# The last node batch of a graph convolution begins two steps earlier, in finer pieces

## The chip, the cores and the metric

The kernel runs on one core of a Trainium2 chip. The metric is the time of one execution in device microseconds, given as the median of several runs. The engines are TensorE (PE, with its weight loads PEld), VectorE (DVE), ScalarE (ACT), GpSimd (POOL) and SyncE (SP), which issues most DMAs. Each engine works its own instructions in order; semaphores join them.

## The reference

A graph network layer: two convolutions over 200,000 edges and 6,250 nodes with 128 features, then attention over the same edges. The edges are sorted by target node.

```python
def mesh_conv(x, src, dst, ea, w1, b1, g, bt, w2, b2):
    m = jnp.concatenate([x[dst], x[src], ea], axis=-1) @ w1 + b1
    m = jax.nn.silu(group_norm(m, g, bt))
    m = m @ w2 + b2
    out = jax.ops.segment_sum(m, dst, num_segments=n)
    cnt = jax.ops.segment_sum(jnp.ones((dst.shape[0],), m.dtype), dst, num_segments=n)
    return out / jnp.clip(cnt, 1.0)[:, None]

h = mesh_conv(x, src, dst, edge_attr, c1_w1, ...)                 # convolution 1
h = jax.nn.silu(group_norm(h, n1_g, n1_b))
h = h + (jax.nn.silu(t_emb) @ tm_w + tm_b)
h = mesh_conv(h, src, dst, edge_attr, c2_w1, ...)                 # convolution 2
h = jax.nn.silu(group_norm(h, n2_g, n2_b)) + x
...                                                               # attention over the edges
```

The targets are drawn as the whole part of 6250 u^2, u uniform from 0 to 1, and sorted.

## The kernel before

**Chunks and steps.** The edges are cut into 196 chunks of 1024 (the last holds 384). A convolution goes over them in the 197 steps of `pipeline`. In each step several chunks are under way. `fetch` of chunk n+2 loads its part of the table of targets (`pk`) and of the relative targets (`ohT`, one DMA for two chunks) on SP, and gathers the table of sources with eight indirect DMAs on POOL into one of four buffers `g`. `products` of chunk n+1 multiplies on TensorE (L1166, into `m`). `first` of chunk n adds the gathered rows on VectorE (L1173), squares on ScalarE (L1175) and reduces the squares on VectorE (L1177). `compared` of chunk n+2 makes the one-hot rows on ScalarE (L685, L686). `second` of an earlier chunk normalises it with three VectorE multiplies and adds (L1188, L1191, L1192), applies SiLU on ScalarE (L1193) and sums the edges by node on TensorE (L1198, into `u`); two masked copies on ScalarE (L1203) and an add on VectorE (L1208) bring the sums into the table `U` in a later step. The root of the variances (ScalarE L1184, reciprocal on VectorE L1274) is taken for two chunks together, which makes odd and even steps differ, and for one chunk at a time in the last steps.

**Node batches.** When all edges of a window of nodes are summed, the nodes themselves can be worked. A batch is four windows of 128 nodes, and `conv_nodes` is its work, as a generator: each `yield` ends its part of one step, and `go_on` resumes it once in each step. `plan_batches` lists the steps in which batches begin, every eighth step, and beside each the chunk whose window number bounds what is finished then. In convolution 1 there are 14 batches, in steps 81, 89, ..., 169, 177, 185. In order, a batch scales the sums (five VectorE instructions, L948 to L955), transposes and copies them (L898, L908), multiplies by the convolution's second weight (L914), adds the bias and squares (L963, L919), reduces the variance (L967), waits for the shared root, scales by it (L925), then idles. After that it transposes again and applies the SiLU (`turned`, L898 and L906), and for each of two weights multiplies (L914), copies (L1007) and stores to the tables `b_d` and `a_d` of the next convolution (L1002, L1012). All batches but the last have six empty steps between L925 and the transposes; the last has none.

Every product and transpose of a batch goes through one PSUM bank, `nd`, which has a single buffer.

**Order.** The order of the instructions on VectorE, ScalarE, TensorE and SP is the order in which the program writes them: `in_order` pins it. In the last 24 steps of a convolution (`early`, n over 172) a batch's part stands ahead of `compared` and `second` in its step, except the parts for variance and scaling, which stand at its end. `products` of the next chunk comes before the batch's part, `second` after it.

**The end of a convolution.** After step 196, `mend` redoes batches that the plan couldn't cover (a loop of zero passes where there are none), and `last_nodes` does the nine last windows of nodes. The next convolution's gathers read the whole table `b_d` and so wait for these nodes.

Of the kernel before, what the change touches and what calls it, by code (L numbers as in the profile page):

```python
# [11 lines left out]
AF = mybir.ActivationFunctionType  # L12
# [19 lines left out]
BN = 4  # L32
# [18 lines left out]
def kernel(ctx: ExitStack, tc: tile.TileContext, x, src, dst, eat, w, out):  # L51
# [9 lines left out]
    nc = tc.nc  # L61
# [106 lines left out]
    NWD = max(0, (NW - 8) // BN * BN)  # L168
    fix_i = {i: const.tile([1, 2], I32, name=f"fix_i{i}") for i in (1, 3)}

    def by_node(table_d, wi, m):
        return table_d[wi * P:(wi + m) * P, :].rearrange("(w p) c -> p w c", p=P)
# [24 lines left out]
    with tc.tile_pool(name="node0", bufs=1) as np_, tc.tile_pool(name="prep", bufs=1) as pp, \  # L197
# [3 lines left out]
        A = h0  # L201
# [43 lines left out]
        for a in range(0, NW, 4):  # L245
            m = min(4, NW - a)
# [12 lines left out]
            tp = pst.tile([P, 4, P], FP, name="tp")  # L259
            for i in range(m):  # L260
                nc.tensor.transpose(tp[:, i, :], A[:, a + i, :], ident)
            tT = np_.tile([P, 4, P], FP, name=f"tT{a}")
# [4 lines left out]
            b = rt.tile([P, 4, D], FP, name="b0")  # L267
# [21 lines left out]
        for a, (m, tT) in keep.items():  # L289
# [3 lines left out]
            b = rt.tile([P, 4, D], FP, name="a0")  # L293
            nc.scalar.copy(b[:, :m, :], o[:, :m, :])
            last = nc.sync.dma_start(out=by_node(a_d[1], a, m), in_=b[:, :m, :])
# [47 lines left out]
    cols = {n: hpc.tile([P, 1], FP, name=f"k_{n}") for n in ("n1_g", "n1_b", "n2_g", "n2_b", "tm_b")}  # L343
# [12 lines left out]
    def steps_of(i):  # L356


        ends, due, n = {}, {}, 0
        for m in spread(i):  # L360
            ends[n + m] = list(range(n, n + m))
            due.setdefault(n + m + (i == 3 or n < NCH - SOON), []).extend(ends[n + m])
            n += m
        waiting, todo, left = [], [], NCH
        while left:
            n = len(todo)
            waiting += due.get(n, ())
            steps = min([m for m in due if m > n], default=n + 1) - n
            k = -(-len(waiting) // steps)
            todo.append(waiting[:k])  # L370
            waiting = waiting[k:]
            left -= k
        return ends, todo

    def plan_batches(i):

        ends, todo = steps_of(i)
        out, done = [], 0
        for n, now in enumerate(todo):
            done += len(now)  # L380
            if n % 8 == (4 if i == 3 else 1) and n > (40 if i == 3 else 80) and n + 6 < NCH \
                    and (i == 3 or n + 5 in ends):
                out.append((n, max(done - 3, 0)))
        return out if NWD else []

    plans = {1: plan_batches(1), 3: plan_batches(3)}
    plans[2] = plans[1]
    at_i = {i: const.tile([1, max(len(plans[i]), 1)], I32, name=f"at_i{i}") for i in (1, 3)}

    for i in (1, 3):  # L390
        plans[i] = plan_batches(i)
# [494 lines left out]
    class Nodes:  # L886
# [11 lines left out]
                nc.tensor.transpose(tp[:, j, :], t[:, j, :], ident)  # L898
            return tp[:, :m, :]

        def turned(self, t, m, tag="x", silu=None):

            tp = self.in_bank(t, m)
            out = self.tile(m, tag)
            if silu:
                nc.scalar.activation(out, tp, AF.Silu, bias=cols[f"{silu}_b"], scale=cols[f"{silu}_g"])  # L906
            else:
                nc.scalar.copy(out, tp)  # L908
            return out

        def times(self, tT, m, rhs):
# [23 lines left out]
    def rows_of(table_d, w, m):  # L935
        at = bass.ds(w * P, m * P) if not isinstance(w, int) else slice(w * P, (w + m) * P)
        return table_d[at, :].rearrange("(w p) c -> p w c", p=P)

    def span(w, m):
        return bass.ds(w, m) if not isinstance(w, int) else slice(w, w + m)  # L940

    def conv_nodes(b, i, w, m, idle=0, last=False):


        at = span(w, m)
        c = b.pool.tile([P, 2, BN], FP, name="n_c")
        if i == 1:
            nc.vector.tensor_scalar(c[:, 0, :m], U[:, at, D], 1.0, None, ALU.max)  # L948
            nc.vector.tensor_scalar(c[:, 1, :m], U[:, at, D], 1.0, None, ALU.min)
            nc.vector.reciprocal(c[:, 0, :m], c[:, 0, :m])  # L950
            nc.vector.tensor_copy(cnt[:, :, at], c[:, :, :m])
        else:
            nc.vector.tensor_copy(c[:, :, :m], cnt[:, :, at])
        st = b.tile(m, "x")
        nc.vector.tensor_tensor(st, U[:, at, :D], c[:, 0, :m, None].to_broadcast([P, m, D]), ALU.mult)  # L955
        yield
        tT = b.turned(st, m)
        yield
        o = b.times(tT, m, squares[f"c{i}_w2"])
        yield  # L960
        A = b.tile(m, "A")
        for j in range(m):
            nc.vector.scalar_tensor_tensor(  # L963
                A[:, j, :], rows[f"c{i}_b2"], c[:, 1, j:j + 1], o[:, j, :], ALU.mult, ALU.add)
        sq = b.squares_of(A, m)
        yield "var"
        nc.vector.tensor_reduce(b.var(), sq, AX.X, ALU.add)  # L967
        yield "root"
        if i == 1 or last:
            b.inverse(A, m)  # L970
            h0T = b.in_bank(h0[:, at, :], m) if i == 2 else None
            yield
            for _ in range(idle + 2 * (idle > 0)):
                yield
            tT = b.turned(A, m, "t", silu=f"n{i}")
            if i == 2:
                nc.vector.tensor_tensor(tT, tT, h0T, ALU.add)
        else:
            b.scaled(A, m, f"n{i}_g", f"n{i}_b")
            yield  # L980
            nc.scalar.activation(A, A, AF.Silu)
            yield
            nc.vector.tensor_tensor(A, A, h0[:, at, :], ALU.add)
            yield

            for _ in range(idle):
                yield
            nc.sync.dma_start(out=rows_of(h2_d, w, m), in_=A)
            tT = b.turned(A, m, "t")
        yield  # L990
        if i == 1:
            ends = ((wab[2][:, D:], None, b_d[2]), (wab[2][:, :D], None, a_d[2]))
        else:
            ends = ((qkv_t[:, 1, :], "kb", kv_d[:, :D]), (qkv_t[:, 2, :], "vb", kv_d[:, D:]),
                    (qkv_t[:, 0, :], "qb", a_d[3]))
        done = None
        for rhs, bias, d_ in ends:
            o = b.times(tT, m, rhs)
            if bias:
                yield  # L1000
            if done:
                nc.sync.dma_start(out=rows_of(done[0], w, m), in_=done[1])  # L1002
            t = b.tile(m, "o")
            if bias:
                nc.vector.tensor_tensor(t, o, rows[bias][:, None, :].to_broadcast([P, m, D]), ALU.add)
            else:
                nc.scalar.copy(t, o)  # L1007
                yield
            done = d_, t
        if bias:  # L1010
            yield
        nc.sync.dma_start(out=rows_of(done[0], w, m), in_=done[1])  # L1012
        if i == 2 and last:
            nc.sync.dma_start(out=rows_of(h2_d, w, m), in_=b.turned(tT, m))
# [58 lines left out]
    def nodes_of(b, i, w, m, hx=None):  # L1073
        return attention_nodes(b, w, m, hx) if i == 3 else conv_nodes(b, i, w, m, last=hx is not None)
# [53 lines left out]
    def conv(i):  # L1128
# [6 lines left out]
        with ExitStack() as es:  # L1135
# [17 lines left out]
            nodes = Nodes(np_of(np_, "A", "o"), lambda: nd.tile([P, BN, D], FP, name="nd", tag="nd"))  # L1153
# [56 lines left out]
            class Stage:  # L1210
                ahead, soon = 2, True
                sums, late, roots, next = [], [], False, 0
                var, j, sd = None, 0, None
# [68 lines left out]
                def batch(self, j):  # L1282
                    w = nc.values_load(at_i[1][0:1, j:j + 1], engines=[DVE, SP], min_val=0,
                                       max_val=max(NWD - BN, 0), skip_runtime_bounds_check_because=WHY)
                    for r in conv_nodes(nodes, i, w, BN, idle=4 if j + 1 < len(plans[i]) else 0):
                        self.roots |= r == "root"
                        yield r

# [53 lines left out]
    with ExitStack() as es:  # L1342
# [22 lines left out]
        nodes = Nodes(np_of(pool("np", 1)), bank)  # L1365
# [135 lines left out]
        class Stage:  # L1501
            ahead, soon = 2, False
            sums, late, nb = [], [], None
            lg, j = None, 0
# [98 lines left out]
        n = NW - NWD  # L1603
# [87 lines left out]
```

## Time and profile before

| | |
|---|---|
| time, median of 3 runs | 6164.96 us (6163.35 to 6166.92) |
| the profiled execution's own time | 6177.55 us |
| its span, first to last instruction | 6175.8 us |
| granted TensorE clock, mean | 0.75 |
| busy: VectorE, POOL, PE, ScalarE | 4994.3, 4487.6, 3615.7, 3353.9 us |
| instructions | 68330 |

In the profile, L-numbers are lines of the kernel. A row of a timeline gives start, duration, engine, line, operation, output and inputs, the count, and in brackets how long the engine had been idle before and what ended that. The last edge sums of convolution 1 (L1198) start at 2055.18 us, and the first gather of convolution 2 at 2079.42.

### The profile page before, as it was taken

Reading aid. Unit: us, or ns where it says so; the run is one execution under the profiler, and the core shown is the slowest. Engines: PE = TensorE matmul, PEld = TensorE weight load, DVE = VectorE, ACT = ScalarE, POOL = GpSimd, SP = SyncE. Lnnn points to the kernel's source line nnn. Section 1 sums busy time; section 2 is a strip of 40 time slices with the busy share of each in tenths; the row PEclk is TensorE's granted clock in tenths of the full one; section 3 lists DMA queues with packets and bytes.
Section 4 is the critical chain, followed back from the end, with each engine's and each line's share of the span. In section 5 each row is a group of like instructions: output and inputs, shape, how many; then the busy total and the mean of one; then the engine's idle time right before and its main releaser. Section 6 shows DMA issues by size and latency. Waiting matters only on the chain. (4 is left out here: it accounts for less than half of the span.)

```text
span 6175.8 us, 68330 instructions
## 1 busy us (share of the span) xinstructions
PE 3615.7 (59%) x20941; PEld 3418.9 (55%) x20942; DVE 4994.3 (81%) x7118; ACT 3353.9 (54%) x5295; POOL 4487.6 (73%) x4706
## 2 busy tenths in 40 slices
PE   5555556556556455565565656555655666666555
PEld 4555555555555455555555555544555555555555
DVE  7888888888888578777888888856778888888877
ACT  5666666666666566666666666632333333333354
POOL 5777777777777577777777777757777777777772
PEclk8777667777777677777777787766778777777776
DMA  6444344444433333343344444445566666666652
GB/s 160 116 127 121 96 115 105 102 108 107 107 101 101 80 100 96 100 101 100 102 114 114 109 112 108 112 121 146 152 157 162 165 166 163 163 166 162 165 150 62
DMA packets 391221, 758.87 MB, mean 123 GB/s; under 512 B 89647, under 2 KB 256946, under 8 KB 361441
## 3 DMA queue, kind: packets, MB, share of 16 engines
q0 software_dynamic: 175056, 410.03, 25.9%
q1 hardware_dynamic: 210144, 340.73, 21.0%
q10 hardware_dynamic: 5632, 3.50, 0.2%
q8 instruction: 173, 2.83, 0.2%
q14 instruction: 216, 1.77, 0.1%
HBM read 707.34 MB, written 46.58 MB: 122 GB/s over the span
## 5 line engine op out<-in xcount | busy, mean ns | idle before, releaser
L718 POOL DMA_INDIRECT g<-b_d,src_i x3126 | 2970.9, 950 | 963.4 <-issue 915.5
L1198 PE MATMUL u<-h,oh 128*128 128x129 f32 (+1 forms) x6252 | 1266.3, 384 | 1435.0 <-ACT h L1193 1434.9
L1198 PEld LDWEIGHTS u<-h,oh 128*128 128x128 f32 x6252 | 1169.3, 288 | 1517.1 <-ACT h L1193 1512.6
L718 POOL DMA_INDIRECT g<-kv_d,src_i x1563 | 1490.7, 954 | 494.6 <-issue 446.4
L1166 PE MATMUL m<-pk,ohT 101*128 101x128 f32 x6252 | 943.2, 315 | 206.4 <-DVE h L1173 161.9
L1166 PEld LDWEIGHTS m<-pk,ohT 101*128 101x128 f32 x6252 | 909.7, 231 | 227.3 <-DVE h L1173 180.7
L1173 DVE TENSOR_TENSOR h<-m,g 128x1024 f32<-128x1024 f32 x392 | 476.4, 1215 | 519.4 <-DMA g<-b_d,src_i 496.0
L1452 PE MATMUL us<-v,oh 128*128 128x145 f32 x3126 | 593.1, 359 | 385.4 <-DVE flat L1477 340.6
L1376 PE MATMUL qe<-pk,ohT 101*128 101x136 f32 x3126 | 567.1, 352 | 373.7 <-ACT ebs L1393 364.1
L1452 PEld LDWEIGHTS us<-v,oh 128*128 128x128 f32 x3126 | 549.8, 250 | 425.6 <-DVE flat L1477 239.6
L1376 PEld LDWEIGHTS qe<-pk,ohT 101*128 101x128 f32 x3126 | 525.0, 252 | 406.5 <-ACT ebs L1393 399.8
L1193 ACT ACTIVATE h<-h 128x1024 f32<-128x1024 f32 x392 | 413.0, 1054 | 594.4 <-DVE h L1192 578.9
L1175 ACT ACTIVATE sq<-h 128x1024 f32<-128x1024 f32 x392 | 411.7, 1050 | 527.9 <-DVE h L1173 526.0
L685 ACT ACTIVATE ohT<-ohT,minus_p 96x1024 f32<-96x1024 f32 x588 | 669.2, 1138 | 17.0 <-DMA ohT<-rel_d 16.5
L686 ACT ACTIVATE ohT<-ohT 96x1024 f32<-96x1024 f32 x588 | 619.8, 1054 | 18.7
L1177 DVE TENSOR_REDUCE var<-sq 128x64 f32<-128x1024 f32 x392 | 475.0, 1212 | 104.5 <-ACT sq L1175 104.4
L1191 DVE TENSOR_TENSOR h<-h,cps 128x1024 f32<-128x1024 f32 x392 | 477.1, 1217 | 13.5
L1192 DVE TENSOR_TENSOR h<-h,cps 128x1024 f32<-128x1024 f32 x392 | 477.0, 1217 | 13.4
L733 DVE TENSOR_TENSOR oh<-cps,dm 128x1024 f32<-128x1024 f32 x392 | 474.2, 1210 | 2.1 <-PE u L1198 2.1
L1188 DVE TENSOR_TENSOR h<-h,cps 128x1024 f32<-128x1024 f32 x392 | 473.7, 1208 | 0.0
L1391 DVE TENSOR_TENSOR g<-qe,g 128x768 f32<-128x768 f32 (+1 forms) x391 | 251.1, 683 | 235.0 <-DMA g<-kv_d,src_i 234.6
L1465 ACT ACTIVATE us<-d 128x16 f32<-128x16 f32 x196 | 36.7, 187 | 660.0 <-DVE d L1461 605.6
(286 smaller groups left out, 4270.6 us busy)
## 6 DMA issues: line engine op xcount, KB each, us to landing
ohT<-rel_d SPq DMA_DIRECT2D x291, 768.0 KB
g<-b_d,src_i POOLq DMA_INDIRECT x3126, 2.5
pk<-a_d SPq DMA_DIRECT2D x588, 46.0 KB
g<-kv_d,src_i POOLq DMA_INDIRECT x1563, 3.0
ohT<-in_eat_dram SPq DMA_DIRECT2D x291, 40.0 KB
a_d<-n_o SPq DMA_DIRECT2D x28, 256.0 KB
kv_d<-n_o SPq DMA_DIRECT2D x28, 256.0 KB
n_h<-h_d SPq DMA_DIRECT2D x19, 256.0 KB
```

The lines of the kernel that those rows point to most:

```text
L685: nc.scalar.activation(k.ohT[:WN, :], k.ohT[:WN, :], AF.Square, bias=minus_p[:WN])
L686: nc.scalar.activation(k.ohT[:WN, :], k.ohT[:WN, :], AF.Relu, bias=1.0, scale=-4.0)
L718: h = nc.gpsimd.indirect_dma_start(out=g[:, t, :table_d.shape[1]], out_offset=None, in_=table_d, in_offset=bass.IndirectOffsetOnAxis(ap=k. ...
L733: return nc.vector.tensor_tensor(k.oh[:, :k.nt, :], iota[:, None, :].to_broadcast([P, k.nt, P]), k.dm[:, :, None].to_broadcast([P, k.nt, P ...
L1166: nc.tensor.matmul(k.m[:, t, :], lhsT=lhs[:, t * P:(t + 1) * P], rhs=rhs, start=(j == 0), stop=(j == len(terms) - 1))
L1173: nc.vector.tensor_tensor(k.mt, k.m[:, :n], k.g[:, :n], ALU.add)
L1177: return lambda: nc.vector.tensor_reduce(var[:, at:at + n * H], sq[:, :n].rearrange("p t (g c) -> p (t g) c", c=HD), AX.X, ALU.add)
L1191: nc.vector.tensor_tensor(k.mt, k.mt, over_edges(gam, k.nt), ALU.mult)
L1192: nc.vector.tensor_tensor(k.mt, k.mt, over_edges(bet, k.nt), ALU.add)
L1198: nc.tensor.matmul(k.u[:, 0, :wide], lhsT=k.oh[:, t, :], rhs=k.h[:, t, :wide], start=(t == 0), stop=(t == k.nt - 1))
L1376: nc.tensor.matmul(k.qe[:, t // TB, at:at + DB], lhsT=lhs[:, t * P:(t + 1) * P], rhs=rhs, start=(j == 0), stop=(j == len(terms) - 1))
L1452: nc.tensor.matmul(k.u[:, :wide], lhsT=k.oh[:, t, :], rhs=k.v[:, t, :wide], start=(t == 0), stop=(t == k.nt - 1))
```

## The change

The last batch of convolution 1 begins two steps sooner (183 instead of 185), and the chunk that bounds its window goes back with it (179 instead of 181). Convolution 2 gets its own plan, which is as it was. `idle` becomes 0 for convolution 1's last batch but one, so that its SiLU follows L925 in the next step; in convolution 2 that batch keeps its 4. A new flag `fine`, set for the last batch of convolution 1 alone, adds a yield between the transposes and the SiLU and one between each product and its copy. To make that possible, `turned` loses its SiLU, which becomes `silu_of`.

```diff
@@ plan_batches
+        if i != 1 or len(out) < 2:
+            return out if NWD else []
+        n = out[-1][0] - 2
+        out[-1] = n, max(sum(len(now) for now in todo[:n + 1]) - 3, 0)
         return out if NWD else []
 
     plans = {1: plan_batches(1), 3: plan_batches(3)}
-    plans[2] = plans[1]
+    plans[2] = plan_batches(2)
@@ class Nodes
-        def turned(self, t, m, tag="x", silu=None):
+        def turned(self, t, m, tag="x"):
 
             tp = self.in_bank(t, m)
             out = self.tile(m, tag)
-            if silu:
-                nc.scalar.activation(out, tp, AF.Silu, bias=cols[f"{silu}_b"], scale=cols[f"{silu}_g"])
-            else:
-                nc.scalar.copy(out, tp)
+            nc.scalar.copy(out, tp)
+            return out
+
+        def silu_of(self, tp, m, n):
+            out = self.tile(m, "t")
+            nc.scalar.activation(out, tp, AF.Silu, bias=cols[f"{n}_b"], scale=cols[f"{n}_g"])
             return out
@@ conv_nodes
-    def conv_nodes(b, i, w, m, idle=0, last=False):
+    def conv_nodes(b, i, w, m, idle=0, last=False, fine=False):
...
             for _ in range(idle + 2 * (idle > 0)):
                 yield
-            tT = b.turned(A, m, "t", silu=f"n{i}")
+            tp = b.in_bank(A, m)
+            if fine:
+                yield
+            tT = b.silu_of(tp, m, f"n{i}")
...
             o = b.times(tT, m, rhs)
-            if bias:
+            if bias or fine:
                 yield
@@ Stage.batch of the convolutions
-                    for r in conv_nodes(nodes, i, w, BN, idle=4 if j + 1 < len(plans[i]) else 0):
+                    for r in conv_nodes(nodes, i, w, BN, idle=(0, 4 * i - 4, 4)[min(len(plans[i]) - 1 - j, 2)],
+                                        fine=i == 1 and j + 1 == len(plans[i])):
```

## The prediction

> **What bounds the kernel now.** I read the page first, then the waits of the end of convolution 1 (from 1880 to 2060 us), then the timelines of the engines there, and last the busy times cut at the steps. From the page:
>
> ```profile
> span 6175.8 us, 68330 instructions
> ...
> L718 POOL DMA_INDIRECT g<-b_d,src_i x3126 | 2970.9, 950 | 963.4 <-issue 915.5
> ```
>
> The gathers of both convolutions take (2970.9 + 915.5) / 3126 = 1.24 us apiece on POOL, eight to a chunk, so 9.95 us a chunk. Over the 196 chunks of a convolution that rate sets the pace. The change touches only the end of convolution 1, so I ask what the pace is there. The waits of 1880 to 2060 us (total, times, longest):
>
> ```profile
> POOL g L718 <- issue: 32.9, 108, 0.3
> ACT n_o L1007 <- PE nd L914: 27.7, 6, 6.5
> ...
> ACT n_t L906 <- PE nd L898: 12.0, 2, 6.1
> ```
>
> POOL runs without a break, and VectorE's sum of products and gathered rows (L1173) is not in the list as waiting for a gather. What is there are eight waits of ScalarE for TensorE in the node batches, together 39.7 us. The step rows show what they cost. I cut the time at each start of L1188, the first normalising multiply of a chunk, counting back from the last full chunk (194, begun at 2045.27, step 196). So the 14 rows are steps 181 to 194; the row of step 190 holds two chunks.
>
> ```profile
> 1887.61:1900.75 13.14, 8.58 (x44) 8.34 (x44) 9.10 (x11) 7.06 (x9) 9.79 (x12) 0.63 0.19 54
> 1900.75:1911.78 11.03, 5.26 (x34) 5.07 (x34) 7.97 (x9) 6.54 (x8) 8.59 (x9) 0.81 0.61 157
> 1911.78:1924.97 13.19, 8.82 (x51) 8.62 (x51) 8.34 (x10) 8.05 (x11) 9.84 (x12) 0.76 0.27 74
> 1924.97:1932.40 7.43, 4.21 (x26) 4.02 (x25) 7.36 (x8) 6.32 (x8) 5.60 (x7) 0.73 0.68 154
> 1932.40:1942.33 9.93, 8.19 (x58) 7.76 (x57) 9.36 (x15) 5.87 (x9) 7.49 (x9) 0.85 0.34 81
> 1942.33:1949.76 7.43, 2.44 (x11) 2.44 (x12) 7.36 (x8) 7.30 (x9) 5.60 (x7) 0.72 0.70 159
> 1949.76:1959.10 9.34, 8.58 (x63) 8.20 (x61) 9.27 (x14) 6.13 (x9) 7.21 (x8) 0.86 0.22 63
> 1959.10:1966.54 7.44, 2.58 (x12) 2.58 (x13) 7.37 (x8) 5.67 (x7) 5.61 (x7) 0.74 0.70 170
> 1966.54:1979.48 12.94, 8.38 (x45) 8.14 (x44) 9.10 (x12) 7.06 (x9) 9.82 (x11) 0.63 0.20 55
> 1979.48:1997.11 17.63, 10.08 (x56) 9.59 (x56) 13.86 (x16) 9.82 (x13) 13.33 (x14) 0.70 0.37 103
> 1997.11:2009.71 12.60, 6.80 (x44) 6.37 (x44) 7.93 (x9) 8.85 (x11) 9.46 (x10) 0.76 0.28 77
> 2009.71:2022.20 12.49, 6.72 (x42) 6.53 (x41) 7.93 (x9) 8.17 (x10) 7.56 (x8) 0.77 0.25 68
> 2022.20:2034.17 11.97, 7.26 (x42) 7.07 (x42) 7.92 (x9) 7.10 (x10) 0.00 (x0) 0.79 0.09 25
> 2034.17:2045.27 11.10, 4.79 (x24) 4.30 (x22) 9.55 (x12) 7.18 (x11) 0.00 (x0) 0.65 0.01 2
> ```
>
> Columns: length, then PE, PEld, DVE, ACT, POOL busy. A step without batch work on TensorE and ScalarE takes 7.44 us when even and 9.34 when odd, and there VectorE is full (7.37 of 7.44). Steps 181 to 183 hold the three last pieces of the batch begun at step 169 (transpose and SiLU, first product and copy, second product and copy) and take 13.14, 11.03, 13.19: 3.8, 3.6 and 3.85 us too much. The batch begun at 177 idles and has the same pieces in 189, 190, 191; the one begun at 185 has them in 191, 192, 193. Step 192 on ScalarE shows the mechanism:
>
> ```profile
> 2013.08 0.59 ACT L1007 COPY n_o<-nd 128x512 f32<-128x512 f32 x1 [4.20 <-PE nd L914]
> 2013.56 1.15 ACT L685 ACTIVATE ohT<-ohT,minus_p 96x1024 f32<-96x1024 f32 x1
> 2014.74 1.06 ACT L686 ACTIVATE ohT<-ohT 96x1024 f32<-96x1024 f32 x1
> 2015.71 0.69 ACT L1203 ACTIVATE u<-u,mask 128x129 f32<-128x129 f32 x2
> 2016.41 1.28 ACT L1193 ACT_TABLE_LOAD   x1
> 2017.71 1.06 ACT L1193 ACTIVATE h<-h 128x1024 f32<-128x1024 f32 x1
> 2018.67 1.04 ACT L1175 ACTIVATE sq<-h 128x1024 f32<-128x1024 f32 x1
> 2019.73 1.28 ACT L1184 ACT_TABLE_LOAD   x1
> 2021.03 0.35 ACT L1184 ACTIVATE sd<-var,eps_t 128x64 f32<-128x64 f32 x1
> ```
>
> The copy waits 4.20 us for a product that stands on TensorE behind the chunk's two big matmul groups, and 4.15 us of in-order work (2013.56 to 2017.71) queues behind the copy, ahead of the chunk's SiLU. In step 194, with no such piece, the SiLU waits only for VectorE:
>
> ```profile
> 2037.92 1.06 ACT L1193 ACTIVATE h<-h 128x1024 f32<-128x1024 f32 x1 [1.40 <-DVE h L1192]
> ```
>
> This gives the undisturbed time of a single-chunk step: 2037.92 - 2034.17 = 3.75 from multiply to SiLU, 2022.20 - 2017.71 = 4.49 from SiLU to the next multiply, 8.24 together.
>
> **The change part by part.** By the yields of the code, the batch of 177 (no idle steps now) does its SiLU in 183, its first product and copy in 184, its second in 185. The last batch begins in 183 instead of 185, transposes and copies in 184, multiplies by the convolution's second weight in 185, and adds the bias in 186. The variance follows in 187, the scaling in 188. Its fine pieces are: transposes 189, SiLU 190, product 191, copy 192, product 193, copy 194, last store 195. No ScalarE instruction of it then sits behind a product of its own step.
>
> Taken away. Step 189 falls from 12.94 to 9.34: 3.6. Step 190 loses a piece whose neighbours cost 3.6 (189) and 12.49 - 8.24 = 4.25 (192): I take 3.7, since like 189 it carries one batch's piece alone. Steps 191 to 193 fall from 12.60 + 12.49 + 11.97 = 37.06 to 3 x 8.24 = 24.72, plus 0.1 for the copy left in 192: 12.2. Is there room on ScalarE for that? Its undisturbed work in a tail step is 4.15 + 3.67 (2017.71 to 2021.38) = 7.82, and 8.3 with the copy, so just. Sum 19.5. The lower end would be that these three steps fall only to POOL's 9.95 us each: 7.2 instead of 12.2, sum 14.5; the higher is 4.25 in each of 189 and 190, sum 20.7.
>
> A rule that speaks against this: the Trainium skill, page "ScalarE: Activation LUTs", section "What ACT_TABLE_LOAD costs", gives each switch of tables about 1.28 us for the load and another 1.38 for a drain. By it, an estimate, two switches a step would make ScalarE's tail step 7.82 + 2.76 = 10.6 us, and 7 us of the gain would be lost. The row is against it: the load at 2019.73 ends at 2021.01 and the root starts at 2021.03.
>
> Put in. In step 183 there is already the last piece of batch 169; the SiLU of 177 comes behind it through the same single bank `nd`:
>
> ```profile
> 2000.55 0.66 PE L898 MATMUL nd<-ident,n_A 128*128 128x128 f32 x4 [0.68 <-ACT n_o L1007]
> ```
> ```profile
> L906 ACT ACTIVATE n_t<-nd,k_n_b,k_n_g x14: 777/777/781, 1011.1 to 2001.8; 128x512 f32<-128x512 f32 x14
> ```
>
> That is transposes after the copy (0.66) and 0.78 for the SiLU: 1.5, between nothing and one more full piece (3.85). Step 184 gets the piece that cost 3.6 in step 182, and behind it through `nd` the last batch's transposes and copy (0.66 + 0.59, less overlap): 4.8, between 3.6 and 3.6 + 3.6 = 7.2. Step 185 gets the piece of step 183, so 13.19 in place of 9.93, plus about 0.4 for the bias adds that now come between it and the next root: 3.7, between 3.3 and 4.3. The five VectorE instructions that begin the batch leave 185 (they are its 9.93 - 9.34) for 183, where VectorE is 8.34 busy of 13.19: nothing. Variance and scaling move from steps in which VectorE waited to 187 and 188, where it is full:
>
> ```profile
> L925 DVE TENSOR_TENSOR n_A<-n_A,n_rs x47: 679/681/714, 939.8 to 6117.6; 128x512 f32<-128x512 f32 x47
> ```
>
> That is 0.7 for the scaling, and 0.3 for the variance, as it takes the place of the bias adds in the 9.34. Sum 11.0, from 8 to 16.
>
> DMA queues. SP's stores of the batch of 177 now stand in 185 and 186, ahead of the loads of later chunks, as they stood in 191 and 192. The last stores go from 193 and 194 to 194 and 195, with only the next convolution's constant rows (L1131) behind them, and its gathers wait for the nodes after step 196 anyway: nothing. The window numbers: the last batch's row now reads chunk 179; targets are 6250 u^2 sorted, and edge 179 x 1024 of 200,000 lies at u = 0.916, node 5250, window 41, over the cap of 40. So the batch covers the same nodes and nothing is redone. Convolution 2 keeps its plan and idles; its SiLU split in two helpers keeps its order.
>
> Can the gain be kept? POOL, from its timeline:
>
> ```profile
> 2006.06 0.95 POOL L718 DMA_INDIRECT g<-b_d,src_i  x1 [0.30 <-issue]
> ...
> 2018.57 0.95 POOL L718 DMA_INDIRECT g<-b_d,src_i  x1 [0.31 <-issue]
> ```
> ```profile
> DMA to landing us min/median/max: 2.4/2.5/9.1
> ```
>
> 2018.57 is the third and last gather of chunk 195, landed at about 2022. Its first use comes after 2034.17, or 2025.7 after a gain of 8.5: not late. Chunk 194's eight gathers begin at 2006.06 and need the buffer of chunk 190, freed before 1997.11. The steps to 188 add 11.0 and 189 gives back 3.6, so 2004.5 at the latest: POOL isn't held up.
>
> Sum: 19.5 - 11.0 = 8.5 us less. The profiled execution took 6177.55 (span 6175.8, 1.75 around it) and would take 6169; it lies 12.6 above the median 6164.96, so the median becomes 6156.5. From the ends, 20.7 - 8 = 12.7 less to 14.5 - 16 = 1.5 more. What this measurement tells from no change is 0.2%, 12.3 us: the forecast lies inside.
>
> **The rivals.** *Slower: the jam at 183 to 185 is dearer than the stalls it replaces.* Two batches share bank `nd` and TensorE's order in these steps. If each of their pieces waits a round behind the big matmuls, with the longest wait seen, 6.5, for both copies of step 184 (13.0), a full piece more in 183 (3.85) and two in 185 (7.5), with the 1.0 of 187 and 188, 25.4 go in: 5.9 more, 6170.9. It decides above 19.5. Against: transposes follow a copy by 0.05 us in the row at 2000.55, with no matmul between. For: no step of the trace has held a copy, transposes and a copy.
>
> *Faster: the pieces of 183 to 185 are hidden.* If the step lengths there stay, 1.5 + 1.2 + 1.0 go in, or 3.7: 15.8 less, 6149. Against: the same pieces cost 3.6 to 3.85 in 181 to 183.
>
> *Returned: another wait takes the place of the stalls.* The tail steps would stay near 12 because of loads or buffers, and 11.0 goes in against 7.3 out or, with half of the tail's gain, 13.4: about no change, 6165. Against: step 194's SiLU had only VectorE to wait for.
>
> *ScalarE's tables bound the tail.* If two switches a step cost more than the spare 8.24 - 7.82 = 0.42, the rest is lost three times; with another load's 1.28 each it is 6.4, leaving 2.1 less: 6163. The row at 2021.03 speaks against it. This is what the rule of the Trainium skill named above would do.
>
> **How the numbers follow.** Forecast 0.74, dearer jam 0.09, hidden pieces 0.08, returned 0.06, tables 0.03. Faster by over 0.2% are the hidden pieces and the forecast's far end: 0.12. Slower by over 0.2% needs a jam twice that of the rival's excess: 0.04. Within: 0.84. The range 6151 to 6166.5 holds the forecast with its ends, the tables and the returned gain; the hidden pieces and the dear jam are left out, 0.17.
>
> **What would show it.** In the changed profile: steps 191 to 193 at 8.2 to 8.6 us and 189 at 9.3, with no ScalarE wait for `nd` after step 185; steps 183 to 185 at 14.7, 12.2 and 13.6; L1188 of chunk 188 about 7 us later than now, of chunk 193 about 8.5 earlier; the first gather of convolution 2 earlier by the same. It is wrong if a tail step stays above 10, if POOL waits for a buffer, or if steps 183 to 185 grow by over 14 together.

## The result, and the profile after

The changed kernel takes 6159.81 us (median of 22 runs), the kernel before 6167.48 in as many: 7.7 us less, a ratio of 0.9986 with a 95% interval from 0.998 to 0.9992. Forecast was 8.5 less, within 0.2% of no change. The forecast of 6156.5 started from a median of 6164.96 in 3 runs; with all 22 the kernel before lies 2.5 higher, so the differences are what to compare. In a later comparison on another chip (below, e6) the ratio was 0.9988 (0.9979 to 0.9997).

The step rows of convolution 1's end again, cut at the start of the same multiply (now L1197), steps 181 to 194; columns as before (length, then PE, PEld, DVE, ACT, POOL busy; the last three are the granted TensorE clock, the DMA share and GB/s):

```profile
1881.66:1894.40 12.74, 8.18 (x44) 7.94 (x44) 9.09 (x11) 7.06 (x9) 9.69 (x11) 0.63 0.21 59
1894.40:1905.23 10.83, 5.06 (x34) 4.87 (x34) 7.98 (x9) 6.54 (x8) 8.09 (x10) 0.82 0.57 156
1905.23:1919.82 14.59, 9.36 (x53) 8.93 (x53) 9.45 (x15) 7.62 (x10) 11.18 (x12) 0.73 0.28 76
1919.82:1932.97 13.15, 6.70 (x39) 6.28 (x39) 7.37 (x8) 7.12 (x9) 9.86 (x11) 0.76 0.54 137
1932.97:1946.28 13.31, 10.09 (x62) 9.72 (x62) 9.28 (x14) 7.86 (x11) 9.96 (x12) 0.78 0.27 77
1946.28:1953.72 7.44, 3.78 (x23) 3.59 (x23) 7.37 (x8) 7.14 (x9) 5.65 (x6) 0.69 0.69 170
1953.72:1963.29 9.57, 7.37 (x54) 6.99 (x53) 9.01 (x12) 6.50 (x9) 7.40 (x8) 0.89 0.22 63
1963.29:1971.24 7.95, 3.09 (x14) 3.10 (x15) 7.88 (x9) 6.67 (x8) 5.82 (x8) 0.68 0.62 160
1971.24:1980.13 8.89, 7.33 (x56) 6.89 (x54) 8.33 (x9) 5.81 (x8) 6.75 (x8) 0.90 0.20 57
1980.13:1994.08 13.95, 7.31 (x35) 7.02 (x36) 13.07 (x14) 9.74 (x14) 10.60 (x12) 0.63 0.35 97
1994.08:2002.52 8.44, 6.17 (x46) 5.98 (x45) 7.93 (x10) 7.57 (x11) 6.31 (x8) 0.87 0.21 60
2002.52:2010.95 8.43, 5.47 (x30) 5.28 (x30) 7.92 (x10) 8.14 (x11) 6.52 (x7) 0.73 0.30 86
2010.95:2019.38 8.43, 5.38 (x46) 5.00 (x45) 7.92 (x9) 6.62 (x11) 3.77 (x4) 1.00 0.15 42
2019.38:2030.33 10.95, 3.65 (x16) 3.46 (x16) 9.56 (x13) 6.77 (x10) 0.00 (x0) 0.69 0.09 26
```

Read from the top: step 183 is a little longer than before, 184 and 185 much longer, 187 and 188 slightly, and from 189 on every step is shorter, the three single-chunk steps 191 to 193 at 8.4 instead of 12. VectorE's busy time in them is unchanged at 7.9: what went is waiting. On ScalarE, step 192 now reads so (timeline):

```profile
2001.60 0.57 ACT L1016 COPY n_o<-nd 128x512 f32<-128x512 f32 x1
2002.06 1.15 ACT L689 ACTIVATE ohT<-ohT,minus_p 96x1024 f32<-96x1024 f32 x1
2003.24 1.06 ACT L690 ACTIVATE ohT<-ohT 96x1024 f32<-96x1024 f32 x1
2004.20 0.69 ACT L1212 ACTIVATE u<-u,mask 128x129 f32<-128x129 f32 x2
2004.91 1.28 ACT L1202 ACT_TABLE_LOAD   x1
2006.27 1.06 ACT L1202 ACTIVATE h<-h 128x1024 f32<-128x1024 f32 x1
```

The copy has no idle time ahead of it; its product was made a step earlier. Step 184 shows what the change put in:

```profile
1923.52 0.58 ACT L1016 COPY n_o<-nd 128x512 f32<-128x512 f32 x1 [4.93 <-PE nd L920]
1924.85 0.58 ACT L909 COPY n_x<-nd 128x512 f32<-128x512 f32 x1 [0.75 <-PE nd L902]
...
1929.47 1.06 ACT L1202 ACTIVATE h<-h 128x1024 f32<-128x1024 f32 x1
```

Two copies through the one bank stand ahead of the chunk's SiLU, the first behind a product, the second 0.75 us behind the transposes. And the first gather of the next convolution, from POOL's timeline, in the kernel before and in the changed one:

```profile
2079.42 0.95 POOL L718 DMA_INDIRECT g<-b_d,src_i  x1 [10.78 <-DMA b_d<-n_o]
```
```profile
2065.67 0.95 POOL L722 DMA_INDIRECT g<-b_d,src_i  x1 [11.84 <-DMA b_d<-n_o]
```

Counted from step 181's start, before to after, that is 2079.42 - 1887.61 = 191.81 against 2065.67 - 1881.66 = 184.01: 7.8 us, close to the difference of the medians. The two profiled executions themselves differ by 16.7 us in span, so only such differences within one profile are used. That 7.8 meets 7.7 so closely is luck: a second trace of the changed kernel (e6) gives 2066.90 - 1887.50 = 179.40. There VectorE waited 3.59 us for a gather in step 182, and steps 181 and 183 took 9.56 and 12.63; from 184 to 193 the two traces agree within 0.2 us a step.

### The profile page after: what moved, and what is told of

Its sections match the earlier page's. It is cut to its first block, busy times and chain, and to the rows that moved or that the text cites. A ratio compares the mean times of both kernels' runs of the same rounds, so it can differ in the third digit from the quotient of the medians.

```text
span 6159.1 us, 68332 instructions
## 1 busy us (share of the span) xinstructions
PE 3609.9 (59%) x20941; PEld 3415.5 (55%) x20942; DVE 4997.3 (81%) x7118; ACT 3354.1 (54%) x5295; POOL 4478.8 (73%) x4706
## 3 DMA queue, kind: packets, MB, share of 16 engines
q8 instruction: 173, 2.83, 0.2%
## 5 line engine op out<-in xcount | busy, mean ns | idle before, releaser
L690 ACT ACTIVATE ohT<-ohT 96x1024 f32<-96x1024 f32 x588 | 619.8, 1054 | 18.7
L1197 DVE TENSOR_TENSOR h<-h,cps 128x1024 f32<-128x1024 f32 x392 | 474.3, 1210 | 0.0
```

Of the source, the lines that this page charges most:

```text
L690: nc.scalar.activation(k.ohT[:WN, :], k.ohT[:WN, :], AF.Relu, bias=1.0, scale=-4.0)
```

## The experiments

Theory A is the prediction's: what costs is a ScalarE piece of a batch that waits for a TensorE product of its own step, because ScalarE's in-order work for the chunk queues behind it. The rivals are B, that an early end of the last batch pays, and C, that the idle steps themselves cost. e1, e2 and e4 tell these apart by parts of the change, e5 and e7 carry the fine pieces further, e6 repeats the change, and e8 alters only TensorE's order. A name with b is the same kernel run again on a second chip.

The kernels were first compared on a chip on which all of them, the kernel before included (7944.92 us), took 29% longer; four results come from there (e1, e2, e4, e5) and are read in the last section. The same kernels were then compared on a chip that ran at the known pace, and these runs decide. Steps are cut in their traces as above.

**e1 and e1b, fine pieces alone.** Of the change, this part only:

```diff
-        if i != 1 or len(out) < 2:
-            return out if NWD else []
-        n = out[-1][0] - 2
-        out[-1] = n, max(sum(len(now) for now in todo[:n + 1]) - 3, 0)
...
-  ... idle=(0, 4 * i - 4, 4)[min(len(plans[i]) - 1 - j, 2)],
+  ... idle=4 if j + 1 < len(plans[i]) else 0,
                                         fine=i == 1 and j + 1 == len(plans[i])):
```

> The last batch begins in step 185 and the batch ahead of it idles, as before; only the fine pieces of the last batch are kept, so that its second copy and both stores come in step 196 and after it. Theory A (what costs is ScalarE standing behind a product of its own step, 3.6 to 4.3 us a piece): steps 189 and 190 stay at 12.9 and 17.6, step 191 keeps one coarse piece (about 12), 192 and 193 fall to 8.3: 8 us less than before, the whole gain of the change. Theory B (what pays is that the last batch is begun and finished sooner): no gain, or up to 10 us more, as its stores come later than before.

> The kernel of e1 again (fine pieces alone), since all kernels of its job, that before included, ran 29% slower than the runs shown, with TensorE standing still between matmuls. Theory A: 8 us less than before, steps 192 and 193 at 8.3, step 191 at about 12. Theory B (an early end of the last batch pays): no gain, or up to 10 us more.

At the known pace: 6160.93 against 6167.49, ratio 0.9991 (0.9982 to 1.0). In its trace, steps 192 and 193 take 8.44 each, 191 keeps the coarse piece of the batch of 177 and takes 13.27. Step 189 missed e1's expectation: it took 9.57, not 12.9. In step 188 VectorE waited 2.80 us for a gather and the step took 10.33, so the two together took 19.90, against 20.38 in the kernel before. So the fine pieces alone bring 6.6 us, nearly what the whole change brings, with a last batch whose second store comes after step 196. The interval reaches 1.0, so this time alone does not exclude B's "no gain"; e4b below does. (On the slower chip: 0.9994, 0.9982 to 1.0007.)

**e2 and e2b, idle steps alone.** `idle=(0, 4 * i - 4, 4)[...]` kept, last batch from 185, `fine=False`.

> Only the idle steps of the last batch but one are taken out; the last batch begins in 185 in coarse pieces as before. Theory A: steps 183 to 185 grow by about 1.4, 3.6 and 3.3, steps 189, 190 and 191 give back 3.6, 3.7 and 0.7: no change within 1 us. Theory C (the idle steps themselves cost): about 8 us less.

> The kernel of e2 again (no idle steps ahead of the last batch, nothing else). Theory A: no change within 1 us, 183 to 185 growing by what 189 to 191 give back. Theory C (the idle steps themselves cost): 8 us less.

At the known pace: 6169.46 against 6167.49, ratio 0.9998 (0.9989 to 1.0007): no change, and C is out: the interval's lower end is 6.8 us less, C has 8. The steps moved about as expected at 183 to 185 (14.68, 11.88, 11.90) and 189 (9.56), but one stall appeared that no theory had:

```profile
ACT n_x L905 <- PE nd L898: 4.6, 1, 4.6
```

The last batch's first transposes, in step 186, waited 0.5 us in the kernel before and cost nothing; behind the jam of 184 and 185 they cost 4.05 (step 186: 11.48 instead of 7.43). And step 191, with the last batch's coarse SiLU, cost nothing: it took 8.46, 4.1 less than before where 0.7 less was expected, and so paid for the stall in 186. That the sum comes out at no change is in part luck. (On the slower chip: 0.997, 0.9956 to 0.9984.)

**e4 and e4b, the change without its fine pieces.** `fine=False` in the changed kernel.

> The change without its fine pieces: last batch from step 183, no idle steps ahead of it, its SiLU in 189, its products and copies in 190 and 191, its last store in 192. Theory A: steps 183 to 185 as in the changed kernel (11 us more than before), 189 and 190 at 12.9 and 17.6 as before, 191 at about 12, 192 and 193 at 8.3: 2 to 3 us more than before. Theory B: as fast as the changed kernel or faster, 8.5 us less than before, as the batch is done three steps sooner than in it.

> The kernel of e4 again (the change without its fine pieces). Theory A: 2 to 3 us more than before. Theory B: 8.5 us less than before, or better.

At the known pace: 6171.69 against 6167.49, ratio 1.0005 (0.9996 to 1.0014), 4 us more where 2 to 3 were expected. The steps: 14.69, 13.21, 13.34 for 183 to 185, 11.89 for 189, 17.40 for 190, 11.95 for 191, 8.43 each for 192 and 193. This is the changed kernel with the gain taken out and the price left in; the last batch is done three steps sooner and nothing is won, so B, which has 8.5 less, is out. Against e1b on the same chip it takes 10.8 us more (6166.1 to 6177.08 against 6156.04 to 6167.42). (On the slower chip: 0.9968, 0.9955 to 0.9982.)

The one combination left, an early start with the idle steps left in, wasn't run: by the code, the coarse last batch would then write its one buffer `n_t` in step 189 while the batch ahead of it still multiplies from it in 190 and 191, and with fine pieces each would wait for the other's use of `nd`.

**e5 and e5b, every batch fine.** Begins and idles as before; the last batch gets three empty steps, so that it meets no other batch in `nd`.

Against the kernel before, with the flag `fine` and its yields put in:

```diff
-  ... idle=4 if j + 1 < len(plans[i]) else 0):
+  ... idle=4 if j + 1 < len(plans[i]) else 2 - i,
+                                        fine=i == 1):
```

> Every batch of convolution 1 in fine pieces; begins and idles as before, but three empty steps for the last batch, whose transposes come in step 194 and whose products and copies come partly after step 196. Theory A: no coarse piece is left, so steps 181 to 194 lie at 7.4 to 9.4 until the gathers bound them; the sum of products and gathered rows then waits for gathers in the last steps, and chunk 195 is taken up about 7 us sooner than in the changed kernel: 15 us less than before. If the drained last batch holds up the last nodes: 3 to 6 us of that are lost. Theory B: slower than before, as the last batch ends last of all.

> The kernel of e5 again (every batch of convolution 1 fine, the last one with three empty steps). Theory A: no step from 181 to 194 over 9.5 us until the gathers bound them, chunk 195 taken up about 7 us sooner than in the changed kernel, 15 us less than before, 3 to 6 less of that if the drained last batch holds up the last nodes. Theory B: slower than before.

At the known pace: 6156.99 against 6167.49, ratio 0.9983 (0.9974 to 0.9992), 10.5 us less. Rows of its waits (1880 to 2060 us):

```profile
DVE h L1178 <- DMA g<-b_d,src_i: 14.1, 7, 3.5
...
DVE n_c L950 <- SPq L742: 6.8, 1, 6.8
```

The first is the floor that was foreseen: VectorE now waits for gathers. They bind earlier than expected: steps 181, 182, 185 and 186 take 10.99, 11.58, 10.62 and 11.07, where none over 9.5 was expected until then. The second row is where some of the gain is lost. What is left of the last batch is drained after step 196: SP issues its last store before it reads the counts of `mend`, and the last nodes wait for that: 39.62 us from the multiply of chunk 194 to the next convolution's first gather, 34.15 in the kernel before. (On the slower chip: 0.9869, 0.9849 to 0.9889, from 5 runs.)

**e6, e7 and e8, on one more chip at the known pace.** e6 is the changed kernel. e7 is e5 with the last batch's first product in 195, and its second product and both copies in 196:

```diff
-        yield
+        if not short:
+            yield
...
-            if bias or fine:
+            if bias or (fine and not (short and done)):
                 yield
...
                 nc.scalar.copy(t, o)
-                yield
+                if not short:
+                    yield
```

e8 is the kernel before with the order on TensorE changed in the last 24 steps of both convolutions, and nothing else:

```diff
-            if n + 1 < NCH and stage.soon:
+            early = stage.soon and n > NCH - SOON
+            if n + 1 < NCH and stage.soon and not early:
                 stage.products(ks[n + 1])
...
             if early:
                 ahead_of = [g for g in under_way if said.get(g) not in ("var", "root")]
                 go_on(n, ahead_of)
+                if n + 1 < NCH:
+                    stage.products(ks[n + 1])
```

> The changed kernel itself, beside the next two on the same chip: 7 to 9 us less than before, chunk 195 taken up about 8 us after its gather has landed.

> As e5, but the last batch multiplies in 195 and does both copies in 196, so that nothing of it is left after step 196. Theory A, with a drain that cost about 5 us in e5: steps 181 to 194 as in e5, the first gather of convolution 2 about 34 us after the start of chunk 194's multiply as in the kernel before (39.6 in e5): 15 us less than before, 7 less than the changed kernel. If the drain was not what held e5 up: about 10 us less, as e5.

> The kernel before, with one thing changed: in the last 24 steps the next chunk's products (2 to 3 us of TensorE) are issued behind the batch's part of the step instead of ahead of it. Batches begin, idle and are cut as before. Theory A: each coarse piece waits 2 to 3 us less on ScalarE (the waits for nd fall from 4 to 6.5 to 1.5 to 4), the eight burdened steps fall by about 2.4 each, until the gathers bound the end: 10 to 15 us less than before. If the pieces cost by ScalarE's own work or by the semaphores between the engines, and not by what stands ahead on TensorE: no change.

The kernel before took 6177.59 us here. e6: 6169.37, ratio 0.9988 (0.9979 to 0.9997). e7: 6161.89, ratio 0.9976 (0.9967 to 0.9985), 15.7 us less, and 7.5 less than e6. e8: 6166.03, ratio 0.9982 (0.9973 to 0.9991), 11.6 us less.

e7's end, from POOL's timeline:

```profile
2016.12 0.95 POOL L718 DMA_INDIRECT g<-b_d,src_i  x1 [0.30 <-issue]
2040.62 5.60 POOL L1136 MEMSET flat<- 128x6600 f32 x1 [23.56 <-PE ln_ps L898]
2057.34 0.95 POOL L718 DMA_INDIRECT g<-b_d,src_i  x1 [11.12 <-DMA b_d<-n_o]
```

Chunk 194's multiply began at 2022.89, 34.45 us ahead of the last row: the drain of e5 is gone, as expected. VectorE took chunk 194 up in the last steps only when its gather had come:

```profile
2014.98 1.23 DVE L1180 TENSOR_TENSOR h<-m,g 128x1024 f32<-128x1024 f32 x1 [0.98 <-DMA g<-b_d,src_i]
```

So the stalls are used up, and convolution 1 ends at the pace of its gathers. e8 shows the cause itself. Its waits of 1875 to 2050 us, against 27.7 in 6 and 12.0 in 2 of the kernel before:

```profile
ACT n_o L1009 <- PE nd L916: 10.1, 5, 3.0
...
ACT n_t L908 <- PE nd L900: 3.2, 2, 2.8
```

The copy of step 192, which waited 4.20 us in the kernel before, now reads:

```profile
2001.35 0.59 ACT L1009 COPY n_o<-nd 128x512 f32<-128x512 f32 x1 [2.06 <-PE nd L916]
```

The pieces are as coarse as they were and take as long on ScalarE; only the group of matmuls ahead of their product went, and with it two thirds of the wait and 11.6 us. What cost was the place in TensorE's order, as A has it. The eight steps with a coarse piece (181 to 183 and 189 to 193) fell by 17.2 us together, unevenly (182 by 0.2, 183 by 4.2), and steps 184 and 188, in which VectorE waited 5.48 and 3.16 us for a gather, grew by 5.6 and 3.3. The gain is not convolution 2's: from its first gather to the first gather of the attention it takes 2009.71 us here and 2009.56 in the kernel before. In e6, chunk 195 was taken up at 2027.78, when its last gather had begun at 2022.28, so with a landing of some 2.5 us after the issue of 0.95 it was taken up about 2 us behind its gather, where 8 were expected, as in the first profile (2026.50 against 2014.92): how near the changed kernel comes to the gathers' floor differs from one execution to the next.

## Why the prediction was right

The steps from 183 to 193, term by term, in the profile after against the profile before:

| term | forecast, us | profile |
|---|---|---|
| step 183, second piece through `nd` | +1.5 | 13.19 to 14.59: +1.4 |
| step 184, product, copy, transposes, copy | +4.8 | 7.43 to 13.15: +5.7 |
| step 185 | +3.7 | 9.93 to 13.31: +3.4 |
| steps 187 and 188 | +1.0 | 9.34 + 7.44 to 9.57 + 7.95: +0.7 |
| step 189 | -3.6 | 12.94 to 8.89: -4.05 |
| step 190 | -3.7 | 17.63 to 13.95: -3.7 |
| steps 191 to 193 | -12.2 | 37.06 to 25.30: -11.8 |
| sum | -8.5 | +11.2 - 19.5 = -8.3 |

The mechanism held in every step of this profile, and no wait of ScalarE for `nd` is left after step 185. Two terms were a little off. In step 184 the piece of step 182 was taken as the price of the first copy, 3.6; but the copy waited 4.93 us here and 4.30 there, as the product group ahead of it on TensorE took 3.01 us here and 2.40 there (before, then after):

```profile
1900.32 2.40 PE L1166 MATMUL m<-pk,ohT 101*128 101x128 f32 x16
1903.65 0.59 ACT L1007 COPY n_o<-nd 128x512 f32<-128x512 f32 x1 [4.30 <-PE nd L914]
```
```profile
1919.58 3.01 PE L1175 MATMUL m<-pk,ohT 101*128 101x128 f32 x16
```

The granted TensorE clock while these groups ran was 0.79 and 0.61, and 0.88 in step 182 of the profile after, where the group took 2.19 us and the copy waited 4.09. So what a piece costs also moves with the clock that its step is granted, and the prediction had no term for that. And the single-chunk step settled at 8.44, not 8.24: SiLU and square of those steps no longer follow each other without a gap (in step 192 the SiLU starts at 2006.27 and the square 1.13 later, 0.96 in the row the 4.49 came from).

After step 194 the profile gives back 1.2 us: 35.34 from chunk 194's multiply to the next gather, 34.15 before. In e1b and e7 it is 33.87 and 34.45, so it is not a price of fine pieces. Nor is it of this execution alone: e6 has 35.30, and e4b, with the early begin and coarse pieces, 35.39. The product group of the last nodes took 2.83 us in the kernel before, at a granted clock of 0.78, and 3.40, 3.32 and 3.52 in these three, at 0.63, 0.65 and 0.60; in e1b and e7 it took 2.88 and 2.92 at 0.75 and 0.74. So a lower clock goes with about half of the loss (0.5 us from that product to the next transposes); why the clock was lower, and where the rest comes from, is open. The prediction put what follows the last stores at nothing. (e8 has 35.67, but there the last nodes' product begins late, 19.33 us after the multiply instead of 18.5 to 18.7.)

The tail had the room on ScalarE that the sum claimed. From the copy at 2001.60 to the same point a step later it is 8.43 us, and ScalarE is busy 8.17 of them; the steps without a copy are as long, so the 0.1 for it was not needed. A table's load is followed by the next instruction at once, as in the row that the prediction shows. The rule of the Trainium skill ("ScalarE: Activation LUTs", "What ACT_TABLE_LOAD costs") that adds a drain of 1.38 us to each switch would, by an estimate, have made such a step 10.6; the measured steps exclude it here.

Of the rivals, the dear jam did not come, but e2b shows that it can: a stall appeared in 186 that the kernel before did not have, worth 4 us, because a step that was harmless stood behind two that were not. "Hidden pieces" fell with step 184. "Returned" did not come: steps 191 to 193 take 8.4 us each in the changed kernel, and in e5b and e7 too. The wait that comes next is that for the gathers, as foreseen, but it held VectorE in the steps before 190, in e1b, e6 and e8 as well, and in the last steps only for chunk 195 in e5b (0.73 us) and for chunk 194 in e7 (0.98).

What the prediction did not ask is which part of the change earns. Its own table would have told: 8 of the 19.5 us taken away (192 and 193) belong to the fine pieces, and the other two parts, 11.5 taken away against 11.0 put in, cancel. e1b, e2b and e4b give this as 6.6 less, 2 more and 4 more, each with an interval of some 5.5 us either way.

## What to carry to other kernels

On an engine that works in order, price a piece of side work not by its own length but by what it waits for and what queues behind the wait: here a 0.59 us copy cost 3.6 to 4.3 us. Splitting it so that producer and consumer fall into different steps, or issuing its producer ahead of the large groups on the other engine, takes most of the price away (15.7 and 11.6 us here); moving it to another step only moves the price, and may stall a neighbour that was free. Before such work is planned, find the floor behind it (here the gathers, which bind in e7, 15.7 us below): it tells when to stop.

## What the runs showed that was not expected

On the chip of the first comparison the kernel before took 7945 instead of 6167 us. VectorE and ScalarE were busy as long as ever (4999.6 and 3374.7 us in e1, 4994.3 and 3353.9 in the kernel before at the known pace), TensorE for 4001.2 instead of 3615.7, at a granted clock of 0.67 instead of 0.75. The trace of e1 there has TensorE standing still between the matmuls of one group, waiting for nothing that the profile shows (waits of the whole execution):

```profile
PEld m L1171 <- issue: 650.5, 446, 35.1
PE m L1171 <- issue: 589.7, 404, 34.8
```

In convolution 1 of the kernel before at the known pace these rows are absent, and the gathers bound it. There, the gathers themselves waited 511.8 us in 88 times for VectorE's sum, which frees their buffers (L1178, 60 to 2560 us of e1), so the steps bound it. One fine batch in fourteen gave nothing that could be measured, while fine pieces in all fourteen batches gave 93 us by the medians (7852.01 in 5 runs against 7944.92; the ratio on record is 0.9869). The ends of convolution 1 agree: POOL cleared the table for the next one at 2565.30 in e1 and at 2472.01 in e5.

```profile
2565.30 5.60 POOL L1134 MEMSET flat<- 128x6600 f32 x1 [53.05 <-PE ln_ps L898]
```
```profile
2472.01 5.60 POOL L1134 MEMSET flat<- 128x6600 f32 x1 [49.87 <-DVE n_x L957]
```

Why TensorE stood still there, what the lower clock has to do with it, and why e2 and e4 came out 0.3% faster on that chip, is open; no trace of the kernel before was taken there.
